# Second group's queries and keys in two banks with chains in turn, and the last three attention outputs scaled by VectorE

## The chip, the cores and the metric

The kernel runs on one core of one Trainium2 chip. The metric is the device time of one execution in microseconds (us), lower is better. A core has a matrix engine (TensorE, PE in the profile; its weight loads are the row PEld), a vector engine (VectorE, DVE), a scalar engine (ScalarE, ACT), a general engine (GpSimd, POOL) and a queue engine (SyncE, SP) that issues most transfers. Matrix products land in PSUM, which this kernel uses as two single banks of 128x512 fp32 (`bank0`, `bank1`) and three pairs of banks (`wide0` to `wide2`). All data are fp32 apart from a few bf16 helpers.

## The reference

Two transformer-like layers on `x` of shape (2, 1024, 512). Each layer is normalised and then adds two branches to `x`. The part that the change touches is the attention branch of the second layer:

```python
xn = _layernorm(x)
x = x + L1_attn(xn) + L1_ffn(xn)

def L1_attn(x):                                  # 16 heads of 32, causal
    q, k, v = split(x @ W_qkv.T + b_qkv, 3)      # per head
    scores = where(causal, q @ k.T / sqrt(32), -inf)
    out = softmax(scores) @ v
    return out @ W_out.T + b_out
```

The first layer's branches (a low-rank scan and a gated network with a Hadamard transform) and the second layer's gated network with 2:4 sparsity run before and behind the attention and are the same in both kernels.

## The kernel before, in words

The program is one list of instructions per engine. A dependency added behind every recorded instruction keeps each of the four compute engines in the order in which the Python code called it, so what a function calls first is first in its engine's queue. Waits between engines are put in by the tile layer from reads and writes of tiles.

**Stages.** The first layer fills about the first 657 us of the span, the attention stage runs from there to about 1215 us, and the gated network of the second layer fills the rest.

**Attention units.** The 16 heads of two sequences are worked in eight units `u` = 0 to 7, each with one sequence and four heads (a group). Per unit there are:

- `project(u)`: queries and keys of the unit, by a seven-product scheme in place of eight. `part(n)`, n = 0 to 6, is two 128x512 products (four PE rows of the trace, line 1122) into one of three chains: `b` (n = 0), `a` (n = 1, 2, 3, 4) and `c` (n = 5, 6). A chain keeps accumulating in its bank, and after every part the bank's present content is written or added to one quarter of `qk[u, 0]` or `qk[u, 1]`: `first` writes it with the bias on ScalarE (line 1087), `more` adds it on VectorE (line 1092). The next part of the same chain must wait until that read is done. Part 0 also makes GpSimd change a weight quarter that part 6 reads.
- `maxima(u, qt, c)`: scores of one block of 128 queries, four products of 32 rows (line 1169) into two wide pairs; VectorE adds the mask (line 1176) and takes the row maxima (line 1177).
- `weights(u, j, kt)`: scores again, transposed (line 1226), less the maxima (line 1232), exponential on ScalarE (line 1243), the causal edge zeroed by GpSimd or, near the end, by VectorE (line 1248).
- `gather(u, j, kt)`: products with the values (line 1272, tile `o`), and the running sums of the weights (line 1279), by GpSimd, near the end by VectorE.
- `total(u, j)` and `divide(u, j, q)`: the sum over keys (line 1291), its copy to the tile `inv` on ScalarE (line 1296; the tile has one buffer), four reciprocals on VectorE (line 1301), and the output `att[u, j]` times `inv` on GpSimd (line 1303).
- `project_out(m)`: output projection (line 1047, tile `po`), added to `x` on VectorE (line 1313).

**Order around the first edit.** The loop over `n` starts at -13. In each step it calls one `maxima`, then `one_part` of what is due, then the fixed work. Unit 0 is projected ahead of the loop (`ps_wide` pairs, part order 1, 0, 2, 5, 3, 6, 4). Unit 1's parts follow, in the order 0 to 6, between the maxima of unit 0, and after them the pieces of the values `values(0, n, j)` (line 1047, tile `pv`). Both take their bank from `next_bank`, which for `n` < 0 alternates: bank 1, bank 0, bank 1, and so on, with a counter `alone`. So before the change unit 1's chains are b in bank 1, a in bank 0, c in bank 1, and the first piece of the values, `pv` (0, 0, 0), is in bank 0. The fixed work of these steps normalises the rows of the other sequence: statistics on VectorE (lines 1000 and 1001), `nm_l` (line 119, VectorE), the two scaled rows `z` on ScalarE (line 123), then transposes on PE (`pt_d`, line 132).

**Order around the second edit.** In the last unit the edge masks and running sums are VectorE's (`idle_vector`), and GpSimd has only three products `att` * `inv` left: (6, 1), (7, 0) and (7, 1). Behind these in GpSimd's queue stand the four weight sums of the next stage's first unit, `combine_w` (lines 173 to 176, tiles `s_c`). Their tiles take the room of attention tiles that are no longer in use.

Of the kernel before, what the change touches and what calls it, by code (L numbers as in the profile page):

```python
# [35 lines left out]
def two_layers(ctx: ExitStack, tc: tile.TileContext, t: dict, out: bass.AP):  # L36
    nc = tc.nc
# [28 lines left out]
    def ps_pair(name, which):  # L66

        return ps.tile([P, 2, 512], F32, tag=f"wide{which}", name=name)

    def ps_wide(name):  # L70
        nonlocal wides
        wides += 1
        return ps_pair(name, wides % 3)

    def ps_bank(name, which):

        return ps.tile([P, 512], F32, tag=f"bank{which}", name=name)
# [278 lines left out]
    with tc.tile_pool(name="a", bufs=1) as a:  # L356
# [431 lines left out]
        for n in range(NU - 1):  # L788
            u = 2 * n + 2
# [143 lines left out]
        n, order = NU - 1, (0, 2, 1, 3, 4, 5, 6)  # L933
# [18 lines left out]
    with tc.tile_pool(name="b", bufs=1, reuse_waits="tile") as b:  # L952
# [73 lines left out]
        att = {}  # L1026
        units = [(bb, hg) for bb in range(B) for hg in range(HG)]
# [3 lines left out]
        def next_bank(name):  # L1031


            nonlocal alone
            if alone is not None:
                alone += 1
            return ps_bank(name, 1 if alone is None else alone % 2)
# [37 lines left out]
        def project(u):  # L1075


            bb, hg = units[u]
            got = {}

            order = (1, 0, 2, 5, 3, 6, 4) if u == 0 else range(7)

            def place(m, n):
                return qk[u, m][:, n * TT : (n + 1) * TT]

            def first(m, n, bank):
                nc.scalar.activation(
                    place(m, n), bank, AF.Identity, bias=bqk[:, m * HG + hg : m * HG + hg + 1]
                )

            def more(m, n, bank):
                nc.vector.tensor_add(place(m, n), place(m, n), bank)

            def weight_sums(w11, w21, w22):

                got[1], got[2] = (
                    sums.tile([P, 2, P], F32, tag=f"sq{n}", name=f"sq{n}_{u}") for n in (1, 2)
                )
                nc.gpsimd.tensor_add(got[1], w21, w22)
                nc.gpsimd.tensor_sub(got[2], got[1], w11)  # L1100
                nc.gpsimd.tensor_sub(w21, w11, w21)

            def part(n):
                x, y = xt1[2 * bb], xt1[2 * bb + 1]
                t1, t2, t3, t4 = tts[bb]
                w11, w12, w21, w22 = (
                    wqk[hg][:, 2 * e : 2 * e + 2, m, :] for m in range(2) for e in range(2)
                )
                if n == order[0]:
                    if (u, 0) not in qk:  # L1110
                        for m in range(2):
                            qk[u, m] = b.tile([P, S], F32, tag=f"qk{m}", name=f"qk{m}_{u}", bufs=3)
                    weight_sums(w11, w21, w22)
                chain = "bbaaaacc"[n + 1]
                lhs = (w12, w11, got[2], w21, w22, got[1], w12)[n]
                rhs = (x[:, 2:, :], x[:, :2, :], t2, t3, t4, t1, y[:, 2:, :])[n]
                start, stop = n in (0, 1, 5), n in (0, 4, 6)
                if start:
                    name = f"pq_{u}_{chain}"
                    got[chain] = ps_wide(name)[:, 0, :] if u == 0 else next_bank(name)  # L1120
                for k in range(2):
                    nc.tensor.matmul(  # L1122
                        got[chain], lhs[:, k, :], rhs[k] if type(rhs) is list else rhs[:, k, :],
                        start=start and k == 0, stop=stop and k == 1, skip_group_check=True,
                    )
                do, *at = (
                    (more, 0, 0), (more, 0, 0), (first, 0, 1), (more, 1, 1), (first, 1, 0),
                    (more, 1, 1), (more, 0, 1),
                )[n]
                if n == order[0] or n == 3 and not got.get("c") or n == 5 and u == 0:  # L1130
                    do = first
                do(*at, got[chain])
                if n == 0:
                    nc.gpsimd.tensor_sub(w12, w12, got[2])

            return [(part, n) for n in order]

        def values(bb, n, j):
# [145 lines left out]
        inv = {}  # L1284
# [13 lines left out]
        def divide(u, j, q):  # L1298

            r = inv[u, j][:, q * P : (q + 1) * P]  # L1300
            nc.vector.reciprocal(r, r)
            if q == 3:
                nc.gpsimd.tensor_mul(att[u, j], att[u, j], inv[u, j])

        def load_out():
            nonlocal wout
# [46 lines left out]
        for u in range(len(units)):  # L1353

            for half in range(2):
                n = per * u - ahead + (3, 11)[half]
                if half and u == len(units) - 1:
                    n -= 1
                if half:
                    put(n + 1, larger, u)  # L1360
                for m in range(3):
                    put_mid(n + 2 + m, shift_part, u, half, m)
                (put_mid if half and u == len(units) - 1 else put_after)(n + 5, shift_rows, u, half)
            if u:
                lo = max(per * (u - 2) - 1, -ahead)
                if u == HG:
                    lo += 3
                rest.append((lo, per * u - ahead - 1, u))
            if u > 1:
                put(max(per * (u - 2) - 4, -ahead), load_qk, units[u][1])  # L1370
            for j in range(2):

                n = per * u + 8 * j + 7
                if (u, j) == (len(units) - 1, 0):
                    n -= 2
                if n < len(second):
                    sums_at.append((n, total, u, j))
                    for q in range(4):
                        put(n + q * 2 // 3, divide, u, j, q)
                else:  # L1380
                    put(len(second) + 1, total, u, j)
        for what in sums_at:
            put_after(*what)
        rest = [(lo, hi, project(u)) for lo, hi, u in rest]
        for n in (0, 1, 4, 5):
            put(per * 2 + n, next_sums)
# [51 lines left out]
        def what_is_fixed(n):  # L1438
            for f, *args in fixed.pop(n, ()):
                f(*args)  # L1440
                if f == total:
                    for q in range(4):
                        put(n + 1, divide, *args, q)
# [15 lines left out]
        for f, n in project(0):  # L1459
            f(n)  # L1460
# [23 lines left out]
        n = len(second)  # L1484
# [13 lines left out]
    with tc.tile_pool(name="c", bufs=1, reuse_waits="tile") as c_:  # L1498
        units = [(pb, g, half) for pb in (1, 0) for g in range(G) for half in range(2)]
# [130 lines left out]
        for n in range(groups - 1):  # L1630

            end = n == groups - 2
            u = 2 * n + 2
# [23 lines left out]
        n = groups - 1  # L1657
# [141 lines left out]
```

## Time and profile before

| what | value |
|---|---|
| median of three runs | 1802.37 us (1801.5 to 1805.26) |
| the profiled execution, its own time | 1803.46 us |
| its span, first to last instruction | 1801.7 us |
| outside the span in that execution | 1.76 us |
| mean granted TensorE clock | 0.998 |
| busy in the span: PE, DVE, POOL, ACT | 1776.1, 1141.5, 847.8, 480.2 us |
| POOL `att` * `inv`, line 1303, 128x512 | 16 times, 1268 ns median |
| ACT `qk` from a bank with bias, line 1087 | 687 ns |
| DVE `qk` plus a bank, line 1092 | 688 ns |
| POOL `s_c`, line 173, 128x512 | 1264 ns median |

A row of the timeline of the trace gives start and duration in us from the span's start, the engine, the line of the kernel, the operation with what it writes and reads, how many instructions are merged, and in brackets how long the engine had been idle before it and which instruction's end it waited for. "issue" stands where no wait is seen. The weight loads (PEld) run beside the products. A 128x512 fp32 product stands in the trace as two rows, each next one starting 0.43 us after the last. Table rows of windows give the length of the window, then busy time and number of instructions of PE, PEld, DVE, ACT and POOL, the granted TensorE clock, and the share and rate of transfers.

### The profile page before, as it was taken

Reading aid. Unit: us, or ns where it says so; the run is one execution under the profiler, and the core shown is the slowest. Engines: PE = TensorE matmul, PEld = TensorE weight load, DVE = VectorE, ACT = ScalarE, POOL = GpSimd, SP = SyncE. Lnnn points to the kernel's source line nnn. Section 1 sums busy time; section 2 is a strip of 40 time slices with the busy share of each in tenths; the row PEclk is TensorE's granted clock in tenths of the full one; section 3 lists DMA queues with packets and bytes.
Section 4 is the critical chain, followed back from the end, with each engine's and each line's share of the span. In section 5 each row is a group of like instructions: output and inputs, shape, how many; then the busy total and the mean of one; then the engine's idle time right before and its main releaser. Section 6 shows DMA issues by size and latency. Waiting matters only on the chain.

```text
span 1801.7 us, 19007 instructions
## 1 busy us (share of the span) xinstructions
PE 1776.1 (99%) x7354; PEld 910.9 (51%) x7354; DVE 1141.5 (63%) x1502; ACT 480.2 (27%) x687; POOL 847.8 (47%) x741
## 2 busy tenths in 40 slices
PE   9999999999999999999999999999999999999999
PEld 5456566555555564333333333334555555555555
DVE  4875444555544457566666666762867778778676
ACT  3322222122221113433433433422212211212220
POOL 5145553355642244577868866613243344342510
PEclk9999999999999999999999999999999999999999
DMA  6120110111101010000000000011110102211101
GB/s 234 47 82 24 49 45 25 35 35 35 35 24 35 12 41 13 1 12 13 1 24 25 13 12 1 25 47 35 35 59 28 54 24 70 84 34 47 47 1 47
DMA packets 29609, 68.12 MB, mean 38 GB/s; under 512 B 3408, under 2 KB 11856, under 8 KB 27984
## 3 DMA queue, kind: packets, MB, share of 16 engines
q1 hardware_dynamic: 28800, 66.61, 11.1%
q8 instruction: 59, 0.97, 0.2%
q10 hardware_dynamic: 720, 0.30, 0.1%
q14 instruction: 30, 0.25, 0.0%
HBM read 62.70 MB, written 4.19 MB: 37 GB/s over the span
## 4 chain that ended last, share of the span: by engine, by line
PE 90%; POOL 4%; DVE 3%; ACT 1%; issue 1%; POOLq 0%; ACTq 0%; DVEq 0%
PE p_a L183 22%; PE p_c L183 21%; PE d L309 19%; PE m L1169 4%; PE s L1226 3%; PE pv L1047 3%; PE po L1047 3%; PE o L1272 3%; POOL acc L1279 3%; PE pq_a L1122 2%; PE dr L1620 2%; PE pq_c L1122 1%; DVE tops L1177 1%; PE pp L607 1%; PE pw L443 1%
## 5 line engine op out<-in xcount | busy, mean ns | idle before, releaser
L327 POOL TENSOR_TENSOR x<-x,de 128x512 f32<-128x512 f32 x87 | 126.6, 1469 | 297.8 <-DVE x L322 162.5
L1279 POOL TENSOR_TENSOR acc<-acc,pt 128x1024 f32<-128x1024 f32 (+3 forms) x138 | 233.7, 1717 | 0.0
L1177 DVE TENSOR_REDUCE tops<-m 128x2 f32<-128x1024 f32 (+2 forms) x192 | 180.9, 956 | 52.3 <-PE m L1169 47.7
L322 DVE TENSOR_TENSOR x<-x,d 128x512 f32<-128x512 f32 x145 | 99.2, 685 | 143.2 <-PE d L309 142.9
L1243 ACT ACTIVATE pt<-s 128x1024 f32<-128x1024 f32 (+3 forms) x160 | 115.4, 766 | 191.1 <-PE s L1232 174.3
L309 PE MATMUL d<-td,h 128*128 128x256 f32 x592 | 139.2, 379 | 0.0
L309 PEld LDWEIGHTS d<-td,h 128*128 128x128 f32 x592 | 112.5, 190 | 42.6 <-issue 28.7
L183 PE MATMUL p_a<-xt,s_a 128*128 128x512 f32 x256 | 116.6, 598 | 0.0
L183 PE MATMUL p_a<-xt,w 128*128 128x512 f32 x256 | 115.4, 593 | 0.7 <-ACT xt L136 0.7
L183 PE MATMUL p_c<-xt,gu 128*128 128x512 f32 x256 | 115.7, 592 | 0.0
L183 PE MATMUL p_a<-t_a,s_a 128*128 128x512 f32 x256 | 115.3, 594 | 0.0
L183 PE MATMUL p_c<-xt,s_c 128*128 128x512 f32 x256 | 115.1, 592 | 0.0
L1169 PE MATMUL m<-qk,qk 32*128 32x512 f32 (+3 forms) x768 | 104.8, 542 | 4.1 <-ACT acc L1243 3.0
L1176 DVE TENSOR_TENSOR m<-m,mask 128x256 f32<-128x256 f32 x128 | 54.8, 428 | 84.3 <-PE m L1169 76.1
L1226 PE MATMUL s<-qk,qk 32*128 32x512 f32 (+3 forms) x768 | 98.2, 532 | 3.5 <-DVE tops L1177 2.3
L176 POOL TENSOR_TENSOR s_c<-gu,s_c 128x512 f32<-128x512 f32 x16 | 20.4, 1274 | 132.4 <-PE p_c L183 132.4
L1169 PEld LDWEIGHTS m<-qk,qk 32*128 32x128 f32 x768 | 40.4, 184 | 73.6 <-issue 25.0
L183 PEld LDWEIGHTS p_a<-xt,s_a 128*128 128x128 f32 x256 | 47.2, 190 | 57.8 <-issue 57.4
L183 PEld LDWEIGHTS p_c<-xt,s_c 128*128 128x128 f32 x256 | 48.6, 190 | 51.5 <-issue 50.2
L183 PEld LDWEIGHTS p_c<-xt,gu 128*128 128x128 f32 x256 | 48.6, 190 | 51.0 <-issue 49.5
L183 PEld LDWEIGHTS p_a<-xt,w 128*128 128x128 f32 x256 | 48.4, 190 | 50.1 <-issue 47.6
L1226 PEld LDWEIGHTS s<-qk,qk 32*128 32x128 f32 x768 | 34.0, 183 | 78.5 <-issue 67.5
(286 smaller groups left out, 3236.3 us busy)
## 6 DMA issues: line engine op xcount, KB each, us to landing
w<-in_W SPq DMA_DIRECT2D x32, 512.0 KB, 3.5
gu<-in_gu SPq DMA_DIRECT2D x32, 512.0 KB, 3.5
wd<-in_down SPq DMA_DIRECT2D x8, 1024.0 KB, 4.8
x<-in_x SPq DMA_DIRECT2D x16, 256.0 KB, 4.2
w2h<-in_W2q SPq DMA_DIRECT2D x4, 1024.0 KB, 12.0
xr<-in_x SPq DMA_DIRECT2D x16, 256.0 KB, 2.6
wqk<-in_WqkvT SPq DMA_DIRECT2D x16, 256.0 KB, 3.1
out_x<-x SPq DMA_DIRECT2D x15, 256.0 KB, 2.0
```

The lines of the kernel that those rows point to most:

```text
L183: nc.tensor.matmul(pair[:, m, :], a[:, m, k, :], x[:, k, :], start=start and k == 0, stop=stop and k == 1, skip_group_check=True,)
L309: nc.tensor.matmul(out_[:, j, :], lhs[:, q, j * P : (j + 1) * P], rhs[:, q], start=m in (0, 1, 3, 4) and j == q == 0, stop=j == q == 1, sk ...
L322: nc.vector.tensor_add(r, r, out_)
L327: nc.gpsimd.tensor_add(r, r, u2[half])
L1047: nc.tensor.matmul(got[0], lhs(k), rhs(k), start=(k == 0), stop=(k == KC - 1))
L1122: nc.tensor.matmul(got[chain], lhs[:, k, :], rhs[k] if type(rhs) is list else rhs[:, k, :], start=start and k == 0, stop=stop and k == 1, ...
L1169: nc.tensor.matmul(pair[h // 2][:, h % 2, :e], q[rows, qt * P : (qt + 1) * P], k[rows, c * 512 : c * 512 + e], start=True, stop=True,)
L1176: nc.vector.tensor_add(d, d, mask.unsqueeze(1).to_broadcast([P, 2, P]))
L1177: nc.vector.tensor_reduce(out=tops[u][:, c, qt, 2 * p : 2 * p + 2], in_=pair[p][:, :, :e], axis=mybir.AxisListType.X, op=ALU.max,)
L1226: nc.tensor.matmul(pair[h // 2][:, h % 2, s:], k[rows, kt * P : (kt + 1) * P], q[rows, cols], start=True, stop=False,)
L1243: nc.scalar.activation(pt[:, :, s:], pair[p][:, :, s:], AF.Exp, scale=1.0 / math.sqrt(HD))
L1279: eng.tensor_add(acc[:, :, s:], acc[:, :, s:], pt[:, :, s:])
```

## The change

Three edits in the second layer's attention:

1. Unit 1's parts take unit 0's order, 1, 0, 2, 5, 3, 6, 4, and with it the same split of `first` and `more`.
2. Unit 1's chains take fixed banks, a in bank 1, b and c in bank 0, and no longer count in `next_bank`.
3. The last three products `att` * `inv`, (6, 1), (7, 0) and (7, 1), are VectorE's; the first thirteen stay on GpSimd.

```diff
-            order = (1, 0, 2, 5, 3, 6, 4) if u == 0 else range(7)
+            order = (1, 0, 2, 5, 3, 6, 4) if u < 2 else range(7)
...
                 if start:
                     name = f"pq_{u}_{chain}"
-                    got[chain] = ps_wide(name)[:, 0, :] if u == 0 else next_bank(name)
+                    if u == 0:
+                        got[chain] = ps_wide(name)[:, 0, :]
+                    elif u == 1:
+                        got[chain] = ps_bank(name, int(chain == "a"))
+                    else:
+                        got[chain] = next_bank(name)
...
-                if n == order[0] or n == 3 and not got.get("c") or n == 5 and u == 0:
+                if n == order[0] or n == 3 and not got.get("c") or n == 5 and u < 2:
                     do = first
...
             if q == 3:
-                nc.gpsimd.tensor_mul(att[u, j], att[u, j], inv[u, j])
+                eng = nc.gpsimd if 2 * u + j < 2 * len(units) - 3 else nc.vector
+                eng.tensor_mul(att[u, j], att[u, j], inv[u, j])
```

No product, sum or transfer is added or removed. The functions that stand around these lines and that the next section speaks of are:

```python
def next_bank(name):
    nonlocal alone
    if alone is not None:
        alone += 1
    return ps_bank(name, 1 if alone is None else alone % 2)

def combine_w(pool, w1, w2, name):               # w1, w2 loaded long before
    nc.gpsimd.tensor_add(s[0], w2[:, :, :2, :], w2[:, :, 2:, :])
    nc.gpsimd.tensor_sub(s[1], s[0], w1[:, :, :2, :])
    nc.gpsimd.tensor_sub(s[2], w1[:, :, :2, :], w2[:, :, :2, :])
    nc.gpsimd.tensor_sub(s[3], w1[:, :, 2:, :], s[1])
```

In the built programs the order changes as follows. On PE unit 1's parts stand in the new order between the same maxima, and nothing else moves. On ACT four writes to `qk` of unit 1 are in both programs; before, all four stand ahead of the two `z`, and after the change the last of them, from chain a, stands behind the two `z`. On DVE one addition to `qk` of unit 1 moves ahead of the maxima of the fourth block of queries, and the three products with `inv` are added: for (6, 1) and (7, 0) right behind their fourth reciprocal, for (7, 1) one addition to `x` later. On POOL the three products are gone, and the weight sums follow directly on the last small sum of unit 7's maxima (line 1199). SP's order is the same.

## The prediction

> **What bounds the kernel now.** I read the page's busy times and its chain first, then the timeline of the two stretches that the edits touch, then windows of 3.41 us.
>
> ```profile
> PE 1776.1 (99%) x7354; PEld 910.9 (51%) x7354; DVE 1141.5 (63%) x1502; ACT 480.2 (27%) x687; POOL 847.8 (47%) x741
> ...
> PE 90%; POOL 4%; DVE 3%; ACT 1%; issue 1%; POOLq 0%; ACTq 0%; DVEq 0%
> ```
>
> PE is the bound. The change takes no work from it, so it pays only by gaps of PE that close or open.
>
> First stretch, timeline, unit 1's projection (660 to 695 us):
>
> ```profile
> 675.90 1.95 PE L1122 MATMUL pq_a<-t_b,sq 128*128 128x512 f32 x4 [0.94 <-DVE qk L1092]
> ...
> 678.68 1.96 PE L1122 MATMUL pq_a<-t,wqk 128*128 128x512 f32 x4 [0.18 <-issue]
> ...
> 689.12 1.98 PE L1047 MATMUL pv<-wv,xt 128*128 128x512 f32 x4
> ...
> 689.43 0.15 DVE L119 SCALAR_TENSOR_TENSOR nm_l<-mv_l,rs_l 128x2 f32<-128x2 f32 x1
> ...
> 689.62 1.52 ACT L123 ACTIVATE z<-x,nm_l,rs_l 128x512 f32<-128x512 f32 x2 [5.49 <-DVE nm_l L119]
> ...
> 692.26 0.63 PE L132 MATMUL pt_d<-ident,z 128*128 128x128 f32 x4 [0.71 <-DVE tops L1177]
> ```
>
> PE waits 0.94 us for the read of chain a, then a little more; `z` waits for VectorE; the values' first piece starts at 689.12 with no wait.
>
> Second stretch, timeline, last unit:
>
> ```profile
> 1169.77 1.27 POOL L1303 TENSOR_TENSOR att<-att,inv 128x512 f32<-128x512 f32 x1 [11.45 <-DVE inv L1301]
> ...
> 1171.07 0.59 ACT L1296 COPY inv<-w 128x512 f32<-128x512 f32 x1 [2.14 <-POOL att L1303]
> ...
> 1179.74 1.26 POOL L1303 TENSOR_TENSOR att<-att,inv 128x512 f32<-128x512 f32 x1 [8.70 <-ACT pt L1243]
> ...
> 1179.79 1.49 DVE L1248 TENSOR_TENSOR pt<-pt,allowed 128x256 f32<-128x256 f32 x1
> ...
> 1181.34 1.05 PE L1272 MATMUL o<-pt,v 128*32 128x512 f32 x4 [0.36 <-DVE pt L1248]
> ...
> 1189.56 1.12 PE L1047 MATMUL po<-wout,att 128*128 128x512 f32 x2 [0.74 <-DVE x L1313]
> ...
> 1200.30 1.26 POOL L173 TENSOR_TENSOR s_c<-gu 128x512 f32<-128x512 f32 x1
> ```
>
> Here VectorE is nearly full and PE waits for it. Its mask at 1179.79 takes 1.49 us where the median of this line is 0.416: it stands still while GpSimd's product runs, and ends 0.28 us after it. GpSimd's weight sums begin only behind the third product.
>
> **Unit 1's order and banks.** *Gain.* Chains now alternate, so a bank's read has another part or a maxima beside it. Spacing from the trace: 1.72 us per part, 1.81 where a maxima follows, then 0.44, 0.65, 0.86 or 1.07 us for maxima of 128, 256, 384 or 512 keys. From 670.73: part 1; maxima 672.54; part 0 at 672.98; part 2 at 674.70, its read (ACT, done 673.34) long past; maxima 676.51, where it was 677.78; part 5 at 677.16; maxima 678.97; part 3 at 679.83; part 6 at 681.55; maxima 683.36; part 4 at 684.43; maxima 686.24, where it was 688.03. VectorE follows 1.27 us earlier, but one `qk` addition (0.69) is now ahead of the fourth block's mask and top: that block starts on VectorE at 685.31 where it was 686.23. The fifth maxima needs the first half of it, done 687.0, so PE is through at 687.6 where it was 689.1: 1.5 us ahead. GpSimd's weight quarters and SP's loads are ready in both orders.
>
> *Loss.* The first piece of the values comes next. Its counter now starts at zero, so it takes bank 1, and bank 1 was last chain a's. Chain a's last read (part 4) stands on ACT behind both `z`, and `z` waits for `nm_l`, which VectorE makes behind the fourth block's tops. So: block at 685.31, `nm_l` 3.20 later as before, 688.51; `z` 0.19 later, 688.70; both and then the read of 0.69 us: 2.11, 690.81; PE starts at 690.9 where it started at 689.12: 1.78 late. PE stands idle from 687.6 to 690.9, 3.3 us. VectorE goes on, so the 0.71 us wait of `pt_d` and some 0.2 of spacing vanish: both transposes 692.72 to 693.60, second half of the piece 693.60 where it was 692.72. **Net +0.9 us.** Behind it each wait is PE to VectorE or ACT and back, so I let nothing more be caught up.
>
> **Three products to VectorE.** Its running sums of 128x1024 take 1.15 to 1.2 us, of 128x512 0.65, so a product costs 0.65.
>
> *Gain.* (6, 1): product done at 1170.2 instead of 1171.04, so `inv` is copied and (7, 0)'s reciprocals start 0.82 earlier. VectorE is full from there to 1179.5. (7, 0): +0.65 on VectorE, but the mask no longer loses 1.07. Masks end at 1179.95 instead of 1181.28, and the projection behind the `o` products starts at 1181.0 instead of 1182.32: -1.3. (7, 1): PE has products from 1194.74 to the next stage and VectorE idles 2.4 to 2.75 us between additions; nothing.
>
> *Loss.* GpSimd is a queue, and the three products held back what stands behind them. With them gone the four weight sums wait only for loaded weights and for PE: their tiles take the room of values, the binding one that of block kt = 4 of unit 7, whose last reader is the `o` product that ends at about 1181. They now run there, not at 1200.3: four times 1.26 us of reads of SBUF, right beside VectorE's edge masks and running sums, which read two SBUF tensors each. The Trainium skill (SBUF — State Buffer, Who interferes with whom) has the loser blocked for a whole instruction; the mask of 1.49 us shows that once, and two masks at 1155.82 that took 2.41 together beside two GpSimd sums show that the engines then take turns. No row shows four in a row against these sums; bounds: 0 (all hidden) and 4 x 1.26 = 5.0 on VectorE. VectorE has no slack, so I take 4.9. The sums of block 4 then end at 1190.1 (1186.5 before), the masks of block 6 at 1190.8, the addition of `po` 8 at 1193.15 (1189.50 before); PE's next projection waits for that addition and starts at 1193.2 where it was 1189.56. **Net of both: +3.65 us**; without the collision -1.3. The sums are needed at 1218.87, so being early buys nothing.
>
> **The clock.** PE's new gaps are 3.3 us in the first stretch, and about 2.2 and 1.7 us around 1190.
>
> ```profile
> 854.39:857.80 3.41, 2.32 (x28) 1.01 (x28) 2.69 (x4) 0.92 (x3) 3.41 (x5) 1.00 0.00 0
> 857.80:861.22 3.42, 3.42 (x10) 1.03 (x9) 1.60 (x3) 0.35 (x2) 3.42 (x5) 0.50 0.02 5
> ...
> 1178.65:1182.07 3.42, 1.79 (x8) 0.29 (x8) 3.42 (x5) 0.88 (x2) 1.26 (x1) 1.00 0.00 0
> 1182.07:1185.48 3.41, 3.41 (x26) 1.26 (x24) 3.41 (x6) 1.16 (x2) 0.00 (x0) 1.00 0.00 0
> ```
>
> A window in which PE idles 1.09 us is followed by one at half clock (again at 977 us), costing up to 1.7 us; a window with 1.63 idle is not. The skill (TensorE: Matmul & The Clock Gate, Why this matters for your kernels) says no idle gaps over about 3 us. By that rule only the 3.3 us gap costs a window: +1.7. By the first row all gaps do: +3.4; by the last perhaps none. I take the rule, one window, since it lies between the rows.
>
> **Sum.** 0.9 + 3.65 + 1.7 = +6.25 us. The profiled execution would go from 1803.46 (span 1801.7 and 1.76 around it) to 1809.7; it lay 1.1 above the median of the runs, so against 1802.37 I say **1808.6**.
>
> **Rivals.**
> - *A, the sums do no harm* (VectorE keeps precedence, or they start later): 0.9 + 1.7 - 1.3 = +1.3, 1803.7. For: GpSimd's last small sum could come late. Against: it ends at 1158, and both waits are over by 1181.
> - *B, the values' piece isn't held* (`z` is early): -1.5 + 3.65, about +2.2, 1804.6. For: `nm_l` needs only statistics. Against: VectorE takes it in order, behind the fourth block.
> - *C, the change does what it sets out to*, not slower: bank 1 is free when PE comes, and no sum meets a mask: -1.3 - 1.3 = -2.6, 1799.8. It decides if ACT's last read is done by 687.6 and the sums start behind 1190.
>
> **How the numbers follow.** A measurement of this kernel can tell about 0.2%, 3.6 us, from no change: below 1798.8 is faster, above 1806.0 slower. Forecast 0.72, A 0.10, B 0.08, C 0.10. The forecast's own span is 1805.4 (no clock window, part of the collision hidden) to 1812 (two windows or more); nine tenths of it is slower. Of B a little is slower; most of C is within the bound. So slower 0.68, same 0.27, faster 0.05. The range leaves C out and reaches to A: 1803.4 to 1812.
>
> **What would show it.** In the profile after: a wait of PE's first `pv` on ACT `qk`, starting near 690.9, with `qk` behind two `z`; no wait of 0.94 in chain a; four `s_c` sums between 1181 and 1190 on POOL, with masks and running sums of over 1.5 us beside them; `att` products of 0.65 us on DVE; a half-clock window behind 690. If the piece starts before 689, or the sums run past 1192, or VectorE's sums keep 1.2 us beside them, the matching step is wrong.

## The result, and the profile after

The changed kernel takes 1812.8 us, the median of four runs (1810.45 to 1813.2), beside 1801.93 us of four runs of the kernel before. The ratio is 1.0048, with a 95% interval of 1.0036 to 1.006: slower, by more than the 0.2% that a measurement can tell. The prediction had the direction and said 1808.6; it is 4.2 us short, and the range ended 0.8 us too low. The profiled execution took 1812.95 us, with a span of 1811.2 us and a mean granted clock of 0.995 (0.998 before).

The page's row of busy times and its chain:

```profile
PE 1782.4 (98%) x7354; PEld 915.1 (51%) x7354; DVE 1148.1 (63%) x1505; ACT 480.4 (27%) x687; POOL 846.9 (47%) x738
...
PE 90%; POOL 4%; DVE 3%; ACT 1%; issue 1%; POOLq 0%; ACTq 0%
```

PE has the same 7354 products and is busy 6.3 us longer. Three instructions went from POOL to DVE. Work wasn't added, so busy time that grows on PE is products that take longer: mostly the clock, in part products that wait inside a row. The trace records stretches of 3.41 us in which the granted clock was 0.50; they are called half-clock windows below. One that is full of products costs half its length, an estimate of 1.7 us.

The timeline of the first stretch, where unit 1's projection hands over to the values:

```profile
689.92 0.15 DVE L119 SCALAR_TENSOR_TENSOR nm_l<-mv_l,rs_l 128x2 f32<-128x2 f32 x1
...
690.10 1.52 ACT L123 ACTIVATE z<-x,nm_l,rs_l 128x512 f32<-128x512 f32 x2 [8.59 <-DVE nm_l L119]
...
691.53 0.67 ACT L1087 ACTIVATE qk<-pq_a,bqk 128x512 f32<-128x512 f32 x1
692.25 0.30 PEld L1047 LDWEIGHTS pv<-wv,xt 128*128 128x128 f32 x2 [3.40 <-ACT qk L1087]
692.25 2.53 PE L1047 MATMUL pv<-wv,xt 128*128 128x512 f32 x4 [2.57 <-ACT qk L1087]
```

The first `pv` waits 2.57 us for ACT's read of chain a, and that read starts only behind both `z` (690.10 + 1.52). The four rows of `pv` then take 2.53 us where they took 1.98. This execution was 1.56 us late when it came here, so `pv` stands at 690.69 on the clock of the kernel before.

The timeline of the last stretch (the execution is 3.35 us late when it begins):

```profile
1182.98 0.75 DVE L1253 TENSOR_TENSOR pt<-pt,allowed 128x256 f32<-128x256 f32 x2
...
1184.93 2.19 POOL L173 TENSOR_TENSOR s_c<-gu 128x512 f32<-128x512 f32 x1 [23.25 <-PE o L1277]
...
1185.92 2.90 DVE L1253 TENSOR_TENSOR pt<-pt,allowed 128x256 f32<-128x256 f32 x2
1187.20 1.34 POOL L174 TENSOR_TENSOR s_c<-s_c,gu 128x512 f32<-128x512 f32 x1
1188.50 1.45 POOL L175 TENSOR_TENSOR s_c<-gu,gu 128x512 f32<-128x512 f32 x1
1188.74 4.50 DVE L1284 TENSOR_TENSOR acc<-acc,pt 128x1024 f32<-128x1024 f32 x2
1189.90 2.25 POOL L176 TENSOR_TENSOR s_c<-gu,s_c 128x512 f32<-128x512 f32 x1
...
1193.63 0.96 PE L1277 MATMUL o<-pt,v 128*32 128x256 f32 x8 [1.51 <-DVE pt L1253]
...
1195.57 0.67 DVE L1319 TENSOR_TENSOR x<-x,po 128x512 f32<-128x512 f32 x1
...
1196.30 2.08 PE L1047 MATMUL po<-wout,att 128*128 128x512 f32 x2 [1.71 <-DVE x L1319]
...
1198.89 4.44 PE L1047 MATMUL po<-wout,att 128*128 128x512 f32 x6
```

The same masks and running sums before:

```profile
1183.48 0.75 DVE L1248 TENSOR_TENSOR pt<-pt,allowed 128x256 f32<-128x256 f32 x2
1184.15 2.35 DVE L1279 TENSOR_TENSOR acc<-acc,pt 128x1024 f32<-128x1024 f32 x2
```

The pair of masks that lies beside the weight sums takes 2.90 us instead of 0.75, and the pair of running sums 4.50 instead of 2.35. That is 4.30 us on VectorE, and the sums are stretched too (2.19 and 2.25 us against 1.26 alone). The six `po` rows at the end take 4.44 us; at full clock, in the run of the products alone, they take 2.84.

Windows of 3.41 us around both places; the last three columns are granted clock, share and rate of transfers:

```profile
686.72:690.14 3.42, 2.95 (x12) 1.01 (x10) 3.35 (x7) 0.04 (x1) 0.28 (x1) 1.00 0.17 44
690.14:693.55 3.41, 1.30 (x3) 0.68 (x4) 2.95 (x4) 2.05 (x3) 2.49 (x2) 1.00 0.39 115
693.55:696.97 3.42, 3.42 (x11) 2.28 (x10) 1.29 (x2) 0.45 (x1) 0.00 (x0) 0.50 0.00 0
1191.90:1195.31 3.41, 1.18 (x20) 0.29 (x8) 3.41 (x5) 0.77 (x2) 0.25 (x1) 1.00 0.64 190
1195.31:1198.73 3.42, 2.43 (x10) 0.70 (x10) 3.42 (x8) 0.00 (x0) 0.00 (x0) 0.50 0.99 414
1198.73:1202.14 3.41, 3.41 (x10) 1.50 (x5) 0.06 (x1) 0.59 (x1) 0.00 (x0) 0.50 0.04 14
```

A window in which PE is busy for 1.30 us is followed by one at half clock; in the last stretch two in a row follow.

Where the 9.5 us between the two profiled executions lie is read by setting the start of each PE product against the same product before: 1.56 come at 24.5 us, from a half-clock window in code that both kernels share; the first stretch adds 2.36; between the stretches 0.57 are given back, because half-clock windows fall elsewhere; the last stretch adds 6.16; nothing after it. So the edits stand behind 8.5 us of it, where the sum had 6.25.

### The profile page after: what moved, and what is told of

The parts are those of the page before. It is cut to its first block, busy times and chain, and to the rows that moved or that the text cites. A ratio compares the mean times of both kernels' runs of the same rounds, so it can differ in the third digit from the quotient of the medians.

```text
span 1811.2 us, 19007 instructions
## 1 busy us (share of the span) xinstructions
PE 1782.4 (98%) x7354; PEld 915.1 (51%) x7354; DVE 1148.1 (63%) x1505; ACT 480.4 (27%) x687; POOL 846.9 (47%) x738
## 3 DMA queue, kind: packets, MB, share of 16 engines
q1 hardware_dynamic: 28800, 66.61, 10.9%
## 4 chain that ended last, share of the span: by engine, by line
PE 90%; POOL 4%; DVE 3%; ACT 1%; issue 1%; POOLq 0%; ACTq 0%
PE p_a L183 22%; PE p_c L183 21%; PE d L309 19%; PE m L1174 4%; PE s L1231 4%; PE po L1047 3%; PE pv L1047 3%; PE o L1277 3%; POOL acc L1284 3%; PE dr L1626 2%; PE pq_a L1127 2%; DVE tops L1182 1%; PE pq_c L1127 1%; PE w L1296 1%; PE pp L607 1%
## 5 line engine op out<-in xcount | busy, mean ns | idle before, releaser
L1277 PE MATMUL o<-pt,v 128*32 128x512 f32 (+3 forms) x640 | 69.9, 483 | 4.6 <-DVE pt L1253 4.3
```

The source lines that it names most:

```text
L1277: nc.tensor.matmul(po[rows, s:], v[:, rows], pts[h // 2][:, h % 2, s:], start=(kt == 0), stop=last, tile_position=(0, h * HD),)
```

## Experiments

In the tables below, "first" and "last" are what each stretch adds, in the profiled execution, to the start of PE's products against the kernel before; in brackets the half-clock windows in that stretch. The first stretch runs from about 655 to 720 us, the last from about 1160 to 1215 us.

| kernel | first | last | median, before beside it (us) | ratio, 95% interval |
|---|---|---|---|---|
| changed | +2.36 (1) | +6.16 (2) | 1812.8, 1801.93 | 1.0048, 1.0036 to 1.006 |
| order alone | +2.17 (1) | +1.17 (1) | 1805.09, 1803.62 | 1.0007, 1.0001 to 1.0014 |
| products alone | +0.04 (0) | +3.39 (1) | 1809.33, 1803.62 | 1.0028, 1.0021 to 1.0036 |
| changed, `pv` in the other bank | -1.63 (0) | +6.43 (2) | 1807.11, 1803.62 | 1.0024, 1.0016 to 1.0033 |
| changed, last product on GpSimd | +2.40 (1) | -0.91 (0) | 1804.77, 1803.62 | 1.0006, 0.9998 to 1.0013 |
| both mends | -1.66 (0) | -0.91 (0) | 1801.38, 1802.3 | 0.9995, 0.9988 to 1.0001 |
| both mends, again | -1.64 (0) | -0.91 (0) | 1801.51, 1803.69 | 0.9986, 0.998 to 0.9993 |
| changed, again | +2.17 (1) | +6.17 (2) | 1809.91, 1802.3 | 1.0042, 1.0027 to 1.0058 |
| last product on GpSimd, dummy reads | +2.36 (1) | +2.46 (0) | 1806.97, 1802.3 | single run |
| last product on GpSimd, dummy writes | +2.35 (1) | -0.91 (0) | 1805.33, 1802.3 | single run |

**The order alone.** Edits 1 and 2, with edit 3 undone:

```diff
-                eng = nc.gpsimd if 2 * u + j < 2 * len(units) - 3 else nc.vector
-                eng.tensor_mul(att[u, j], att[u, j], inv[u, j])
+                nc.gpsimd.tensor_mul(att[u, j], att[u, j], inv[u, j])
```

> The second unit's two chains in turn, all attention products left on GpSimd as before. The theory (the first pv product waits for the last read of chain a, which stands on ScalarE behind both z): the order gives about 1.4 us at the fifth maxima, then pv starts about 2.3 us later than the first pair's products would let it, and the TensorE's idle time there costs one window at half clock: first stretch +0.9 without that window and +2.3 with it, so 1802.8 to 1804.3 if the kernel before takes 1801.9. The rival (that wait is covered, the order only gives): 1800.5. The last stretch has to run as before: scale sums of the last unit from 1200.3 us plus the shift so far, x + po unchanged against it.

Timeline of this kernel:

```profile
686.81 1.49 PE L1174 MATMUL m<-qk,qk 32*128 32x512 f32 x8
...
690.15 0.67 ACT L1087 ACTIVATE qk<-pq_a,bqk 128x512 f32<-128x512 f32 x1
690.87 3.47 PE L1047 MATMUL pv<-wv,xt 128*128 128x512 f32 x4 [2.57 <-ACT qk L1087]
...
1200.46 1.27 POOL L1308 TENSOR_TENSOR att<-att,inv 128x512 f32<-128x512 f32 x1 [19.23 <-DVE inv L1306]
1201.69 1.27 POOL L173 TENSOR_TENSOR s_c<-gu 128x512 f32<-128x512 f32 x1
```

The same wait of 2.57 us, with no help from the other edit: +1.47 on the medians, inside the 0.9 to 2.4 expected. The weight sums stay at the end, behind the product. The last stretch was to run as before; it adds 1.17 us, with a half-clock window at 1182.0 us where the profile of before has none (PE idles 1.80 us in the window ahead of it, and 1.63 us before). The rival (-1.4) falls.

**The products alone.** Edit 3 on the kernel before:

```diff
-                nc.gpsimd.tensor_mul(att[u, j], att[u, j], inv[u, j])
+                eng = nc.gpsimd if 2 * u + j < 2 * len(units) - 3 else nc.vector
+                eng.tensor_mul(att[u, j], att[u, j], inv[u, j])
```

> The kernel before with only the last three attention products on VectorE. The theory (GpSimd, free of them, starts its four weight sums some 15 us earlier, beside VectorE's masks and running sums, which are held by them): the last stretch is 3.4 us longer by the dependent instructions, and up to 2.8 us more by windows at half clock: 1805.3 to 1808.1 from 1801.9. The rival (the sums hold nothing on the path; what is gained is the reciprocal's room and the masks no longer held): 1800.6 to 1801.0. In the trace: first sum about 1181.5 us by the theory, with masks of 1.4 us and running sums of 2.2 us each beside it. First stretch as before.

Timeline:

```profile
1184.74 1.33 POOL L173 TENSOR_TENSOR s_c<-gu 128x512 f32<-128x512 f32 x1 [25.95 <-PE o L1272]
1184.86 2.89 DVE L1248 TENSOR_TENSOR pt<-pt,allowed 128x256 f32<-128x256 f32 x2
...
1187.68 4.50 DVE L1279 TENSOR_TENSOR acc<-acc,pt 128x1024 f32<-128x1024 f32 x2
...
1195.24 1.13 PE L1047 MATMUL po<-wout,att 128*128 128x512 f32 x2 [1.71 <-DVE x L1314]
```

Masks of 1.45 us and running sums of 2.25 us each, +3.39 in the stretch, +5.7 on the medians: the theory's row. The sums start when the `o` products release their room, as expected, though at 1182.4 rather than 1181.5 on the clock of the kernel before (1184.74 less 2.29), since in this profile those products ran in a half-clock window. The first stretch is untouched (+0.04).

**The first `pv` in bank 0, that of chains b and c.** The changed kernel; only the count of banks moves on by one:

```diff
+        def next_turn():
+            nonlocal alone
+            alone += 1
...
                     elif u == 1:
+                        if n == order[0]:
+                            next_turn()
                         got[chain] = ps_bank(name, int(chain == "a"))
```

> The changed kernel, but the single-bank products after the second unit's chains go on from the other bank, so that the first pv takes the bank of chain b, whose readers are done early, and only the second pv takes that of chain a. The theory: pv starts as soon as TensorE comes to it, about 2.9 us earlier than in the changed kernel; the transposes behind it then wait for z. The changed kernel's first stretch of +2.3 (a window at half clock among it) turns into -1 to 0 and the total into 1809.0 to 1811 from the changed kernel's 1812.8; where the half-clock window stays away, the lower end. The rival (it isn't that bank: the products after pv are held by z all the same and by as much): no change from the changed kernel, within 0.5 us.

Timeline:

```profile
686.53 1.49 PE L1180 MATMUL m<-qk,qk 32*128 32x512 f32 x8
...
687.94 1.98 PE L1051 MATMUL pv<-wv,xt 128*128 128x512 f32 x4
...
688.44 1.52 ACT L123 ACTIVATE z<-x,nm_l,rs_l 128x512 f32<-128x512 f32 x2 [8.59 <-DVE nm_l L119]
...
689.76 1.34 PE L132 MATMUL pt_d<-ident,z 128*128 128x128 f32 x8
```

`pv` follows the maxima with no wait and stands beside `z`; the read of chain a is as late as it was, and nobody waits for it. The first stretch turns from +2.36 to -1.63, without a half-clock window. Against the kernel before, the median is 3.5 us up instead of the 7.6 and 10.9 that the changed kernel showed, so 4.1 or more are won, a little over the 1.8 to 3.8 expected (at the same clock, by the fit below, 1.9 us: 3.54 less 1.67). So it was that bank.

**The last product back on GpSimd.** The changed kernel, with (6, 1) and (7, 0) still on VectorE:

```diff
-                eng = nc.gpsimd if 2 * u + j < 2 * len(units) - 3 else nc.vector
+                eng = nc.vector if (u, j) in ((6, 1), (7, 0)) else nc.gpsimd
```

> The changed kernel, but only two of the three products on VectorE: the last unit's second product is on GpSimd as before, and the four weight sums queue behind it there. The theory: the sums start where they started before (about 1200 us plus the shift), masks and running sums of the last block run at about 0.4 and 1.2 us each, and the last stretch is 0.9 to 1.3 us shorter than before instead of 3.4 us (and the half-clock windows) longer: total 1804 to 1807, from 1812.8 of the changed kernel. The rival (it is VectorE's load of products, not the sums, that makes the last masks late): the two products stay on VectorE, so at least two thirds of the loss stay, 1810 or more.

Timeline:

```profile
1182.82 0.75 DVE L1253 TENSOR_TENSOR pt<-pt,allowed 128x256 f32<-128x256 f32 x2
1183.49 2.35 DVE L1284 TENSOR_TENSOR acc<-acc,pt 128x1024 f32<-128x1024 f32 x2
...
1188.90 1.13 PE L1047 MATMUL po<-wout,att 128*128 128x512 f32 x2 [0.74 <-DVE x L1319]
...
1198.37 1.27 POOL L1309 TENSOR_TENSOR att<-att,inv 128x512 f32<-128x512 f32 x1 [39.80 <-DVE inv L1306]
1199.60 1.27 POOL L173 TENSOR_TENSOR s_c<-gu 128x512 f32<-128x512 f32 x1
```

One product on GpSimd, itself needed late, holds the four sums back by some 18 us (1199.60 - 0.25 against 1184.93 - 3.35 on the clock of the kernel before). Masks and sums have their usual times and the stretch is 0.91 shorter than before. VectorE carries two of the three products and loses nothing by them: the rival falls.

**Reads or writes.** The kernel just shown, with work put in behind the product (7, 0); both variants write a tile that no one reads any more:

```diff
                 eng.tensor_mul(att[u, j], att[u, j], inv[u, j])
+                if (u, j) == (7, 0):
+                    nc.gpsimd.tensor_add(bo[:, :1], att[u, j][:, :1], att[u, j][:, :1])
+                    for _ in range(4):                    # the second variant: range(8)
+                        nc.gpsimd.tensor_add(bo, att[u, j], att[u, j])   # nc.gpsimd.memset(bo, 0.0)
```

> The kernel with the last unit's second product on GpSimd (whose last stretch was 0.9 shorter than before), with five additions put in on GpSimd behind the last unit's first product: one of 128x1, then four of 128x512 that read that product twice and write a tile no one reads any more. They take the place of the four weight sums, from about 1180 to 1190, but need no room and no loads. The theory (VectorE's operations with two inputs in SBUF are held while GpSimd reads SBUF): masks over 1 us and running sums of 128x1024 over 1.8 us each beside them, x + po 2 to 4 us later than without them. The rival (the weight sums held VectorE by something else, their place in the tiles' rooms for instance): masks 0.4, running sums 1.2, last stretch as without them.

> The same place, the same small addition, but behind it eight memsets of 128x512 on GpSimd that write the unused tile and read nothing. The theory (it is the reading that holds VectorE): masks 0.4 and running sums 1.2 us each beside them, last stretch 0.9 shorter than before. The rival (any work of GpSimd on SBUF holds VectorE): as with the additions, in proportion to the time of the memsets.

Timeline with the additions:

```profile
1181.24 6.24 POOL L1313 TENSOR_TENSOR bo_bc<-att 128x512 f32<-128x512 f32 x4
1181.36 4.04 DVE L1284 TENSOR_TENSOR acc<-acc,pt 128x1024 f32<-128x1024 f32 x2
...
1185.33 2.43 DVE L1253 TENSOR_TENSOR pt<-pt,allowed 128x256 f32<-128x256 f32 x2
```

and with the memsets:

```profile
1182.93 4.60 POOL L1313 MEMSET bo_bc<- 128x512 f32 x8
1183.07 2.35 DVE L1284 TENSOR_TENSOR acc<-acc,pt 128x1024 f32<-128x1024 f32 x2
...
1185.34 0.75 DVE L1253 TENSOR_TENSOR pt<-pt,allowed 128x256 f32<-128x256 f32 x2
```

The additions cost VectorE 1.69 us on one pair and 1.68 on the other, and the stretch is 3.37 us longer than without them (+2.46 against -0.91): the whole of what VectorE lost arrives at PE. Eight memsets take 4.60 us in the same place and cost nothing. So GpSimd's reading alone holds VectorE; the sums' loads and rooms aren't needed for it. These additions cost 3.37 us where the weight sums cost 4.30; what the other 0.9 us hangs on wasn't tested.

**The changed kernel again,** the same code beside more runs of the kernel before.

> The changed kernel once more, beside the same runs of the kernel before, to part the instructions' loss from the clock's. The theory (the steps of the sum were right in size, 0.9 and 3.65, and only the clock's share was too small): among runs with the same granted clock the changed kernel is 4.2 to 5.2 us slower, and the rest of the difference of the medians goes with a clock that is lower by 0.001 to 0.003 on average. The rival (the waits themselves cost more than the sum has them): 6 us or more at the same clock, and no lower clock.

Each run lists its mean granted clock, so the instructions' share and the clock's can be parted: over the runs taken together I fitted the time as a line in the clock (listed to 0.001), with one slope for both kernels and an offset between them; ± is its 95% interval.

| kernel | runs, of before | offset at the same clock (us) | mean clock against before |
|---|---|---|---|
| order alone | 22, 62 | +1.03 ± 0.27 | -0.0002 |
| products alone | 14, 62 | +2.99 ± 0.45 | -0.0016 |
| `pv` in the other bank | 15, 62 | +1.67 ± 0.40 | -0.0015 |
| last product on GpSimd | 22, 62 | +0.14 ± 0.29 | -0.0010 |
| changed, again | 7, 28 | +3.54 ± 0.74 | -0.0029 |
| both mends | 22, 28 | -2.71 ± 0.24 | -0.0011 |
| both mends, again | 21, 25 | -3.07 ± 0.32 | -0.0005 |

The slope is 1.3 to 1.55 us for each 0.001. Of the changed kernel's 7.9 us (means), 3.54 are instructions and 0.0029 x 1.49 = 4.4 us are clock. The instructions' share came out a little below the 4.2 to 5.2 expected, reaching it only at the end of its interval; the lower clock is at the end of what was expected. The rival (6 us or more at the same clock) falls. The single edits add up within the intervals: 1.03 + 2.99 = 4.0.

One thing stays open. One full half-clock window lowers the mean clock of a run by 0.0009 (1.7 of 1803 us). The clock of the changed kernel, lower by 0.0029, thus stands for about three windows, as many as its profile has in the two stretches. But the order alone, whose profile has one in each stretch, is lower by only 0.0002 over 22 runs; its profile lacks the windows at 858 and 981 us that the kernel before has. So a window in one place seems to spare one elsewhere at times; why was not tested.

**Both mends.** The first `pv` in the other bank, and the last product on GpSimd.

> Both mends at once: the first pv from the bank of chain b, and the last unit's second product on GpSimd ahead of the weight sums. The theory (the change loses by these two waits and by the half-clock windows behind them, by nothing else): first stretch -1.6 and last stretch -0.9 against the kernel before, as each mend gave alone, and no half-clock window behind either: 1801.1 if the kernel before takes 1803.6, ratio 0.9986. The rival (the order itself or VectorE's two products cost something that the mends leave): 1803 to 1805, ratio 1.000 to 1.001.

Windows of this kernel at both places:

```profile
690.51:693.93 3.42, 3.30 (x18) 1.35 (x11) 3.39 (x6) 2.09 (x3) 1.29 (x2) 1.00 0.52 153
693.93:697.34 3.41, 3.41 (x18) 1.70 (x18) 3.10 (x7) 1.34 (x3) 2.08 (x3) 1.00 0.02 5
...
1183.66:1187.08 3.42, 3.04 (x28) 1.16 (x24) 3.42 (x6) 1.10 (x3) 0.00 (x0) 1.00 0.00 0
```

PE is nearly full and the clock whole. The stretches gain what each mend gave alone, -1.66 and -0.91, and the rival falls on that; but the medians lay only 0.9 us apart, with an interval that includes no change. Hence once more:

> The kernel with both mends once more, since its instructions were 2.6 us shorter than before and the medians only 0.9 apart. If its lower mean clock (0.0011 under that of the kernel before) was chance, the medians are 2 to 3 us apart, ratio 0.9983 to 0.9989. If it lasts, they are about 1 us apart, ratio 0.9995; at the same granted clock it is 2 to 3 us faster either way.

This time the ratio is 0.9986 (0.998 to 0.9993), as first expected. At the same clock the two series agree, -2.7 and -3.1, so this version is shorter than both kernels. Its mean clock was lower than that of the kernel before in both (by 0.0011 and 0.0005), which takes part of the gain back; why is not settled. In the profile of the first series two half-clock windows lie at 23.5 us, long before any changed code.

## Why the prediction came out as it did

**What bounds the kernel: right.** Nothing was added to PE; all that counted were its gaps, and those were the two named.

**The order's gain: right in kind, 1.1 instead of 1.5 us.** In the run of the order alone, PE comes through the fifth maxima at 688.12 on the clock of the kernel before (686.81 + 1.49 - 0.18), where it was 689.20. The start is 1.4 earlier instead of the forecast's 1.8, because parts with no maxima between them follow each other at 1.82 us (680.20 to 682.02 there) where the forecast had 1.72; and these maxima take 1.49 us instead of 1.16, since they wait inside for half of the fourth block.

**The first `pv` in bank 1: right.** Predicted start 690.9, measured 690.69; predicted idle 3.3 us, measured 2.57; some 0.5 of the difference is the smaller gain above, and 0.2 the earlier start. Net 0.9 predicted; at the same clock the order alone costs 1.03 ± 0.27. The other bank removes the wait, so the cause is shown.

**The three products' gain: 0.91 instead of 1.3.** The forecast's own terms, -0.82 + 0.65 - 1.07, come to -1.24, and each was a little off. In the run with the last product on GpSimd the reciprocals of (7, 0) start 0.61 earlier (1171.33 - 0.25, before 1171.69), the masks behind them 0.12 later (1179.88 - 0.25, before 1179.51), so the product cost VectorE 0.73; and the pair of masks takes 0.75 instead of 1.77. That is -0.61 + 0.73 - 1.02 = -0.90.

**The weight sums: right, 4.3 us on VectorE instead of 4.9.** 2.15 on the masks and 2.15 on the running sums; 4.30 - 0.91 = 3.39, which is what `x` + `po` is late in the changed kernel (1195.57 - 3.35 = 1192.22, where it was 1188.82) and what the stretch adds in the run of the products alone. The forecast said 3.65. The Trainium skill (SBUF — State Buffer, Who interferes with whom) has it that a GpSimd operation that reads SBUF contends with a VectorE operation of two SBUF inputs; the dummy reads confirm it, 3.37 us, and the dummy writes show the other side, 0.

**The clock: this is the term that was mis-sized.** "I take the rule, one window, since it lies between the rows", +1.7. The runs show three windows from the two gaps, and 4.4 us by the fit.

In the first stretch one window came, but not for the reason given. The Trainium skill's rule (TensorE: Matmul & The Clock Gate, Why this matters for your kernels: no idle gaps over about 3 us) was applied to a gap of 3.3 us. The measured gap is 2.57 us, which the rule would have passed, and yet all six profiles with this wait have the window and none of the five without it. The right count here was luck.

In the last stretch the waits behind the sums, one of 1.51 us and one of 1.71 across the next border, are followed by two windows in a row in all three profiles that have the sums early and the order changed (changed, again, other bank). Those cost about 6.16 - 3.39 = 2.8 us, and the forecast had counted them as nothing. No gap of PE in the two stretches reached 3 us.

What parts the cases in these two stretches is not the single gap but PE's idle time summed within one window of 3.41 us. With windows laid on the grid on which the half-clock windows of a profile begin, and over all eleven profiles, each of the 11 full-clock windows with 1.80 to 2.57 us of idle PE was followed by a half-clock window, and none of the 13 with 1.25 to 1.79 us was. In the three profiles named, the first wait and the start of the second fall into one window (2.23 to 2.45 us idle). In the run of the products alone they fall into two windows (1.33 and 1.71), with the dummy reads too (1.37 and 1.46), and none follows there. A second half-clock window followed here where PE idled 0.44 to 0.99 us in the first, and not where it idled up to 0.39. So how the gaps fall into windows matters, and the forecast, which took gaps one by one, could not see it. Its row of 1.09 us idle, by which every gap costs a window (+3.4), comes nearer in the sum but is no rule for these stretches: the 13 windows idled longer and lost nothing.

Of the rivals, A falls with the products alone, B with the order alone. C, both edits as meant, is what the two mends make of the change: -2.6 was its sum, -2.57 is what the stretches show. That the two agree so closely is luck, since the terms were -1.3 and -1.3 and came out as -1.66 and -0.91.

## What to carry to other kernels

Taking work off a queue pulls forward what stood behind it: ask what that is and what it reads, before counting the gain. A bank is free when its last reader is done, so look where that reader stands in its engine's order, not when its input is ready. Where PE is the bound, price gaps with the half-clock window that may follow, summing the idle time of neighbouring gaps (in these stretches over 3.41 us), and compare runs at the same granted clock before calling a difference the instructions'.

## What the runs showed that was not expected

The border between 1.79 and 1.80 us of idle time holds in the two stretches alone. In the changed kernel's profile these two windows are neighbours:

```profile
1181.66:1185.07 3.41, 1.62 (x9) 0.59 (x10) 3.38 (x6) 0.81 (x2) 0.14 (x1) 1.00 0.00 0
1185.07:1188.49 3.42, 3.23 (x20) 0.95 (x18) 3.42 (x3) 1.31 (x2) 3.34 (x2) 1.00 0.00 0
```

PE idles 1.79 us and the next window keeps its clock, while windows with 1.09 us idle lost it at 857 us here and at 854 and 977 us before. Nor does 1.09 us decide there: in the profiles of both mends and of the dummy reads, windows with the same idle time at 856 and 855 us kept it. Where the gap lies doesn't settle it either: the quiet gap here (1181.24 to 1183.45) lies across its window's start, but so does the gap of the first `pv` (689.68 to 692.25, window from 690.14), which was followed. The ends of products are modelled in the trace, so hundredths of idle time mean little. What else counts towards the clock is open.

Half-clock windows begin on a grid of 3.413 us: those at 857.80 and 980.68 us before are 36 such steps apart. The grid lies differently against the program in each profile, so one gap can fall into one window or two. That would account for the spread of one and the same kernel: 62 runs of the kernel before lay between 1801.19 us at a clock of 1.0 and 1808.06 us at 0.995.
